# A message-passing layer on one core: one wait a step, transposes two groups ahead, destinations' rows from resident columns

## The chip, the cores and the metric

The kernel runs on 1 core of a Trainium2 chip, in float32 throughout. Five engines run their own instruction streams and meet at semaphores: TensorE (matmuls and transposes, "PE" in the profile, with its weight loads as "PEld"), VectorE ("DVE"), ScalarE ("ACT"), GpSimd ("POOL") and SyncE ("SP"). In this kernel GpSimd issues the indirect loads, and SP and ACT issue the plain ones. The metric is the device time of one execution in microseconds, median of several runs.

## What is computed

A layer of a graph network over 12,500 nodes of 64 features and 212,500 edges of 32 features, which come sorted by destination:

```python
def _mlp(x, W1, b1, W2, b2):
    return jax.nn.relu(x @ W1 + b1) @ W2 + b2
...
msg_in = jnp.concatenate([nodes[row], nodes[col], edge_features], axis=-1)   # 64 + 64 + 32
messages = _mlp(msg_in, mW1, mb1, mW2, mb2)                                  # hidden 128, out 64
aggregated = jax.ops.segment_sum(messages, col, num_segments=nodes.shape[0])
upd_in = jnp.concatenate([nodes, aggregated], axis=-1)
return _mlp(upd_in, uW1, ub1, uW2, ub2)
...
x = _layernorm(x + _L0_gnn_ref(x, src, dst, edge_attr_32, ...), axis=-1)
```

`row` is the source of an edge (`src`), `col` its destination (`dst`).

## The kernel before

The edges are cut into 554 groups of 384 (`G`, `GE`), three tiles of 128 each (`TG`; the last group has only 148 edges, in two tiles). As the edges are sorted by destination, the destinations of a group lie in a window of 32 consecutive nodes (`W`) that begins with the group's first destination. A check on the device confirms that the window holds every edge; if it does not, a slower path (`unordered`) computes everything anew. With these inputs that path does not run.

**The order is written out by hand** (`manual_schedule`): each engine runs its instructions in the order in which the program lists them. The framework adds the waits, from which instruction writes and reads which tile.

A group goes through these functions; the group a step works on is given in brackets for step g of the main loop:

- `gather` (g+16), L93 to L101: three indirect loads on GpSimd's queue, one per tile; each fetches the 64 features of 128 source nodes from HBM into the columns behind a place for a one-hot matrix in the tile `s`. There are 18 buffers of `s` (`AHEAD + 2`), so a gather has to wait until the sums of the group 18 earlier are done. The gathers also take turns on eight semaphores.
- `tables_for` (g+8) and `table`, L180 to L194: a chunk of 512 nodes at a time, the product of the nodes' features and the destinations' part of the first weight matrix (and the bias) is computed by TensorE (L184), copied by ACT (L187) and written to HBM as the table `by_dst` (L188). There are 25 such chunks (`PLAN`).
- `window` (g+4), L269 to L280: SP loads the 32 rows of `by_dst` that belong to the group's window into the first 32 rows of one of six weight tiles `wm`; below them lie, loaded once, the weights for source features (64 rows) and edge features (32 rows). The number of the window's first node is a register's value, which SP and DVE load.
- `onehot` (g+2), L282: DVE compares each edge's destination, relative to the window, with 0 to 31. That gives the one-hot columns of `s`.
- `turn` (g+1), L290: three transposes on TensorE (L298) turn one-hot and source features into columns, in PSUM (`xt`); ACT copies them to SBUF (L299), above the edge features (`st`, loaded by SP for four groups at a time, L262), and adds up how many edges each node of the window has (`counts`).
- `hidden` (g), L302: three matmuls of these 128 rows with `wm` give the hidden layer in PSUM (`pre`, L307). One-hot times table row, source features and edge features are all in the one product. ACT applies the relu (L311).
- `sums` (g−2), L317: a transpose of the counts (L321) and three matmuls of the hidden layer with the one-hot columns (L323) sum it by destination into `sg`.
- `add` (g−2), L328: DVE adds `sg` into the resident sums `agg` (L330) and the counts into row 0 of the resident `xc` (L331), at an address from the register. `xc` holds all nodes' features as columns, with the counts as its row above them.
- `step_update` (g−2), L394: as soon as all edges of a chunk of 512 nodes are through, its update (second weight matrix, update network, layer norm) is done in four parts, one per step.

Every float32 matmul shows in the profile as two passes; a transpose shows as one. In PSUM, `xt`, `pre` and `sg` have two buffers each, one bank a buffer; one more bank is for tables and updates (`u_ps`), one for a constant.

Ahead of the loop stand the loads, the preparation of the windows' starts, the first table chunk, the check, and the clearing of `agg` (L244). The first 48 gathers are issued ahead of all this, since GpSimd's stream has nothing else.

The main loop, quoted in part:

```python
for g in range(G + 2):
    if g < G:
        ...
        gather(g + AHEAD)
        tables_for(g + SOON)
        window(g + NEXT)
        onehot(g + 2)
        turn(g + 1)
        hidden(g)
    if g > 1:
        sg = sums(g - 2)
        step_update(g - 2)
        add(g - 2, sg)
```

Of the kernel before, what the change touches and what calls it, by code (L numbers as in the profile page):

```python
# [19 lines left out]
P = 128  # L20
# [14 lines left out]
NEXT = 4  # L35
# [12 lines left out]
def plan():  # L48


    import math

    def node(g, sign):
        q = min(1.0, g * GE / E)
        return g * GE * N / E + sign * (6.0 * math.sqrt((E - N) * q * (1 - q)) * N / E + 6)

    chunks, b = [], 0
    for e in [c * CH for c in range(1, N // CH + 1)] + [N]:
        opens = next((g for g in range(G) if node(g, 1) + W >= b), G)
        closes = next((g for g in range(G) if node(g, -1) >= e), G)  # L60
        n = e - b
        chunks.append((b, *((P, n // P) if n % P == 0 else (n // 2, 2)), opens, closes))
        b = e
    return chunks
# [6 lines left out]
def ordered(ctx: ExitStack, tc: tile.TileContext, a, ok):  # L71
# [6 lines left out]
    dram = ctx.enter_context(tc.tile_pool(name="dram", bufs=1, space=DRAM))  # L78
    gp = ctx.enter_context(tc.tile_pool(name="gather", bufs=AHEAD + 2))
    stp = ctx.enter_context(tc.tile_pool(name="st", bufs=3))  # L80
    bp = ctx.enter_context(tc.tile_pool(name="bout", bufs=2))
# [9 lines left out]
    gathered = {}  # L91

    def gather(g):  # L93
        s = gp.tile([P, TG, W + D], F32, name="s")
        for j, p in enumerate(tiles_of(g)):
            t = g * TG + j
            nc.gpsimd.indirect_dma_start(  # L97
                out=s[:p, j, W:], out_offset=None, in_=x[:, :],
                in_offset=bass.IndirectOffsetOnAxis(ap=src_sb[:p, t : t + 1], axis=0),
            )  # L100
        gathered[g] = s  # L101
# [14 lines left out]
    zero = const.tile([W, H], F32, name="zero")  # L116
# [5 lines left out]
    xc = const.tile([D + 1, NP], F32, name="xc")  # L122
# [4 lines left out]
    nc.sync.dma_start(xc[0:1, :].rearrange("o (p n) -> o p n", p=P), ones[:, : NP // P])  # L127
    w1b = const.tile([D + 1, H], F32, name="w1b")
    nc.scalar.dma_start(w1b[0:1, :], a["mb1"][None, :])
    nc.scalar.dma_start(w1b[1 : D + 1, :], a["mW1"][D : 2 * D, :])  # L130
    cuts = [0, 3 * CH, 12 * CH, N]
# [3 lines left out]
    NW = 6  # L135
# [9 lines left out]

    lo, hi = np.zeros(G), np.full(G, float(N - 1))
    for base, p, n, opens, closes in PLAN:
        lo[closes:] = base + p * n
        hi[:opens] = np.minimum(hi[:opens], base - W)

    def steps(v):

        at = [0, *(np.flatnonzero(np.diff(v)) + 1).tolist(), len(v)]
        return [(i, j, float(v[i])) for i, j in zip(at, at[1:])]

    bound = temp.tile([1, G], F32, name="bound")

    def set_bound(v):
        for i, j, value in steps(v):
            nc.vector.memset(bound[:, i:j], value)  # L160

    set_bound(hi)
    start_f = temp.tile([1, G], F32, name="start_f")
    nc.vector.tensor_scalar(start_f, first_f[0:1, :], 0.0, None, ALU.max)
    nc.vector.tensor_tensor(start_f, start_f, bound, ALU.min)
# [8 lines left out]


    by_dst = dram.tile([N + W, H], F32, name="by_dst")
    nc.sync.dma_start(by_dst[N:, :], zero)
    tables = list(PLAN)

    def table():  # L180
        base, p, n, _, _ = tables.pop(0)
        ps = ups.tile([H, CH], F32, name="u_ps").rearrange("p (n h) -> p n h", n=4)
        for k in range(n):
            nc.tensor.matmul(ps[:p, k], xc[:, base + k : base + p * n : n], w1b,  # L184
                             start=True, stop=True)
        t = bp.tile([P, 4, H], F32, name="t")
        nc.scalar.activation(t[:p, :n], ps[:p, :n], AF.Copy)  # L187
        nc.scalar.dma_start(  # L188
            by_dst[base : base + p * n, :].rearrange("(p n) h -> p n h", p=p), t[:p, :n])

    def tables_for(g):

        while tables and tables[0][3] <= g:
            table()  # L194

    SOON = NEXT + 4
    tables_for(SOON)

# [18 lines left out]
    nc.tensor.matmul(wps[:, 2, 0:1], u1s, b2, start=True, stop=True)  # L217
# [3 lines left out]

    nc.vector.tensor_tensor(ub1, ub1, wps[:, 2, 0:1], ALU.subtract)
# [8 lines left out]
    wrong = temp.tile([1, 2, G], F32, name="wrong")  # L231
    nc.vector.tensor_tensor(wrong[:, 0], first_f[0:1, :], bound, ALU.is_gt)
    set_bound(lo)
    nc.vector.tensor_tensor(wrong[:, 1], first_f[0:1, :], bound, ALU.is_lt)
    nwrong = temp.tile([1, 1], F32, name="nwrong")
    nc.vector.tensor_reduce(nwrong, wrong, mybir.AxisListType.XY, ALU.add)
# [13 lines left out]
    xtp = ctx.enter_context(tc.tile_pool(name="xt_ps", bufs=2, space=PSUM))  # L250
    prp = ctx.enter_context(tc.tile_pool(name="pre_ps", bufs=2, space=PSUM))
    sgp = ctx.enter_context(tc.tile_pool(name="sg_ps", bufs=2, space=PSUM))
    counts = const.tile([D + W, G], F32, name="counts")

    st, starts, hs = {}, {}, {}
# [13 lines left out]
    def window(g):  # L269
        if g >= G:  # L270
            return
        if g % SB == 0:
            n = min(SB, G - g)
            _, v = nc.values_load_multi_w_load_instructions(
                start_i[0:1, g : g + n], engines=[ET.SP, ET.DVE], min_val=0, max_val=N - 1,
                skip_runtime_bounds_check_because="they were clamped to the nodes on the chip",
            )
            for i in range(n):
                starts[g + i] = v[i]
        nc.sync.dma_start(wm[g % NW][:W, :], by_dst[bass.ds(starts[g], W), :])  # L280

# [8 lines left out]
    def turn(g):  # L290

        if g >= G:
            return
        s = gathered[g]
        t, c, n = columns(g)
        xt = xtp.tile([D + W, GE], F32, name="xt")
        for j, p in enumerate(tiles_of(g)):
            nc.tensor.transpose(xt[:, j * P : j * P + p], s[:p, j, :], ident[:p, :p])  # L298
        nc.scalar.activation(t[: D + W, c : c + n], xt[:, :n], AF.Copy,  # L299
                             accum_out=counts[:, g : g + 1])  # L300

    def hidden(g):  # L302
        t, c, n = columns(g)
        sizes = tiles_of(g)
        pre = prp.tile([P, TG, H], F32, name="pre")
        for j, p in enumerate(sizes):
            nc.tensor.matmul(pre[:p, j, :], t[:, c + j * P : c + j * P + p], wm[g % NW],  # L307
                             start=True, stop=True)
        h = ep.tile([P, TG, H], F32, name="h")
        if len(set(sizes)) == 1:  # L310
            nc.scalar.activation(h, pre, AF.Relu)  # L311
        else:
            for j, p in enumerate(sizes):
                nc.scalar.activation(h[:p, j, :], pre[:p, j, :], AF.Relu)
        hs[g] = h

    def sums(g):  # L317
        h, s = hs.pop(g), gathered.pop(g)
        sizes = tiles_of(g)
        sg = sgp.tile([P, TIMES + 1, W], F32, name="sg")  # L320
        nc.tensor.transpose(sg[0:1, TIMES, :], counts[:W, g : g + 1], ident[:W, :W])  # L321
        for j, p in enumerate(sizes):
            nc.tensor.matmul(sg[:, :TIMES, :], h[:p, j, :],  # L323
                             s[:p, j, :W].unsqueeze(1).to_broadcast([p, TIMES, W]),
                             start=j == 0, stop=j == len(sizes) - 1)
        return sg

    def add(g, sg):  # L328
        at = bass.ds(starts.pop(g), W)
        nc.vector.tensor_tensor(agg[:, at], sg[:, 0, :], agg[:, at], ALU.add)  # L330
        nc.vector.tensor_tensor(xc[0:1, at], sg[0:1, TIMES, :], xc[0:1, at], ALU.add)  # L331

    def update(base, p, n):
# [8 lines left out]
        def first(xin):  # L342
            u_ps = ups.tile([H, CH], F32, name="u_ps")
            nc.tensor.matmul(u_ps[:, :q], wc, agg[:, rows], start=True, stop=False)  # L344
            nc.tensor.matmul(u_ps[:, :q], ux, xc[:, rows], start=False, stop=True)  # L345
            u = up.tile([H, CH], F32, name="u")
            nc.scalar.activation(u[:, :q], u_ps[:, :q], AF.Relu, bias=ub1)
            nc.vector.tensor_tensor(xin[:p, :n], xin[:p, :n],
                                    u2b[:p].unsqueeze(1).to_broadcast([p, n, D]), ALU.add)
            return xin, u  # L350
# [31 lines left out]
    waiting = [(closes, update(base, p, n)) for base, p, n, _, closes in PLAN]  # L382
# [14 lines left out]
    for g in range(NEXT):  # L397
        window(g)
    onehot(0)
    onehot(1)  # L400
    turn(0)
    for g in range(G + 2):
        if g < G:
            if g % SB == 0:
                inputs(g // SB + 2)
            if g + AHEAD < G:
                gather(g + AHEAD)
            tables_for(g + SOON)
            window(g + NEXT)
            onehot(g + 2)  # L410
            turn(g + 1)
            hidden(g)
        if g > 1:
            sg = sums(g - 2)
            step_update(g - 2)
            add(g - 2, sg)
# [331 lines left out]
```

## Time and profile before

| | us |
|---|---|
| median of 3 runs (2108.9 to 2110.22) | 2109.17 |
| the profiled execution | 2528.93 |
| its span, first to last instruction | 2527.2 |
| TensorE's mean granted clock in it | 0.786 of full |
| first gather issued / last gather issued | 2.91 / 2480.53 |

The profiled execution took 420 us longer than the timed ones. The profile and its trace are of that execution.

Some further groups, in the form line, engine, operation, out<-in, shape, count | busy us, mean ns of one | idle time of the engine just before them, and what ended most of it:

```profile
L298 PE MATMUL xt<-ident,s 128*96 128x128 f32 x1661 | 355.4, 335 | 443.8 <-remote 246.7
L299 ACT ACTIVATE st<-xt 96x384 f32<-96x384 f32 x554 | 267.9, 484 | 1002.3 <-PE xt L298 469.4
L330 DVE TENSOR_TENSOR agg<-sg,agg 128x32 f32 x554 | 106.2, 192 | 1899.2 <-PE sg L323 761.2
L184 PE MATMUL u_ps<-w1b,xc 65*128 65x128 f32 (+1 forms) x196 | 54.2, 453 | 112.9 <-DVE xc L331 80.3
```

How to read them: the first says that the transposes of L298 kept TensorE busy for 355.4 us, 335 ns each, and that TensorE stood idle for 443.8 us just before such an instruction, of which 246.7 us ended with something that the trace does not name ("remote"). Idle time of an engine is no loss by itself; it is one only where the end of the kernel hangs on that engine.

### The profile page before, as it was taken

How to read it: one execution, taken by the hardware profiler on the slowest of the kernel's cores; microseconds unless marked ns; L12 is line 12 of the kernel's file. 1: busy time of each engine (PE TensorE's matmuls, PEld its weight loads, DVE VectorE, ACT ScalarE, POOL GpSimd, SP SyncE). 2: the span in 40 equal slices, each digit the busy share in tenths (PEclk: the TensorE clock that was granted, in tenths of full speed). 3: DMA queues.
4: the chain of work that ended last, by engine and by line, in shares of the span. 5: the costliest groups of instructions: out<-in, count | busy, mean ns of one | idle time of the engine just before them, and what ended most of it. 6: DMA issues, size and time to landing. Idle time of an engine off the chain costs nothing.

```text
span 2527.2 us, 31410 instructions
## 1 busy us (share of the span) xinstructions
PE 1697.3 (67%) x9359; PEld 1457.9 (58%) x9359; DVE 392.9 (16%) x2103; ACT 598.2 (24%) x1740; POOL 1570.3 (62%) x1668
## 2 busy tenths in 40 slices
PE   0566767776676776776666766666667676677667
PEld 0455656665565665665555655556566565666556
DVE  3111111111111111111111111111111111111112
ACT  0222222222222222222222222222222222222223
POOL 6666666666666666666666665666666666666661
PEclk9787777777778677777877787788787778787879
DMA  5111111111111111111111111111111111111111
GB/s 127 34 43 46 40 43 45 41 44 43 40 44 41 42 47 39 45 43 40 43 41 42 47 42 40 40 43 44 41 42 47 36 47 40 43 47 38 46 39 28
DMA packets 99895, 111.48 MB, mean 44 GB/s; under 512 B 39997, under 2 KB 65062, under 8 KB 99590
## 3 DMA queue, kind: packets, MB, share of 16 engines
q0 software_dynamic: 53152, 54.51, 9.6%
q1 hardware_dynamic: 41928, 45.07, 6.4%
q10 hardware_dynamic: 4638, 9.80, 1.3%
q8 instruction: 79, 1.29, 0.2%
q14 instruction: 98, 0.80, 0.1%
HBM read 99.55 MB, written 9.62 MB: 43 GB/s over the span
## 4 chain that ended last, share of the span: by engine, by line
PE 66%; another core or an unknown queue 16%; issue 12%; DVE 2%; ACT 1%; DVEq 0%; DMA 0%; ACTq 0%
PE sg L323 25%; PE pre L307 21%; PE xt L298 12%; PE sg L321 2%; PE u_ps L184 2%; PE u_ps L357 2%; PE u_ps L344 1%; PE u_ps L345 1%; ACT st L299 1%; DVE o L374 0%; DVE mv L364 0%; DVE stats L363 0%; DVE xc L331 0%; DVE y L359 0%
## 5 line engine op out<-in xcount | busy, mean ns | idle before, releaser
L97 POOL DMA_INDIRECT s<-in_x,src_sb x1661 | 1569.6, 945 | 910.3 <-issue 420.5
L307 PE MATMUL pre<-wm,st 128*128 128x128 f32 x3322 | 635.3, 343 | 205.1 <-issue 140.3
L307 PEld LDWEIGHTS pre<-wm,st 128*128 128x128 f32 x3322 | 572.1, 254 | 241.7 <-issue 165.3
L323 PE MATMUL sg<-s,h 128*128 128x128 f32 x3322 | 660.4, 348 | 1.8 <-issue 1.8
L298 PE MATMUL xt<-ident,s 128*96 128x128 f32 x1661 | 355.4, 335 | 443.8 <-remote 246.7
L323 PEld LDWEIGHTS sg<-s,h 128*128 128x128 f32 x3322 | 535.6, 240 | 29.2 <-issue 1.7
L298 PEld LDWEIGHTS xt<-ident,s 128*96 128x96 f32 x1661 | 234.3, 159 | 501.7 <-remote 259.2
L299 ACT ACTIVATE st<-xt 96x384 f32<-96x384 f32 x554 | 267.9, 484 | 1002.3 <-PE xt L298 469.4
L311 ACT ACTIVATE h<-pre 128x384 f32<-128x384 f32 x553 | 268.8, 486 | 668.0 <-PE pre L307 257.3
L330 DVE TENSOR_TENSOR agg<-sg,agg 128x32 f32 x554 | 106.2, 192 | 1899.2 <-PE sg L323 761.2
L285 DVE TENSOR_TENSOR s<-iota,dlc 128x96 f32<-128x96 f32 x554 | 141.9, 257 | 54.6 <-issue 53.7
L184 PE MATMUL u_ps<-w1b,xc 65*128 65x128 f32 (+1 forms) x196 | 54.2, 453 | 112.9 <-DVE xc L331 80.3
L184 PEld LDWEIGHTS u_ps<-w1b,xc 65*128 65x128 f32 (+1 forms) x196 | 47.5, 326 | 118.2 <-issue 51.9
L321 PE MATMUL sg<-ident,counts 32*1 32x32 f32 x554 | 107.2, 194 | 0.0
L299 ACT ACTIVATION_READ_ACCUMULATOR st<-xt 96x1 f32 x554 | 106.0, 191 | 0.0
L331 DVE TENSOR_TENSOR xc<-sg,xc 1x32 f32 x554 | 99.2, 179 | 13.9 <-PE u_ps L345 5.3
L321 PEld LDWEIGHTS sg<-ident,counts 32*1 32x1 f32 x554 | 41.1, 74 | 90.2 <-issue 43.9
L357 PE MATMUL u_ps<-u,u 128*128 128x64 f32 (+1 forms) x196 | 49.5, 399 | 20.5 <-issue 11.2
L357 PEld LDWEIGHTS u_ps<-u,u 128*128 128x128 f32 (+1 forms) x196 | 47.1, 324 | 23.2 <-issue 12.2
L344 PE MATMUL u_ps<-agg,wc 128*128 128x512 f32 (+1 forms) x50 | 33.3, 753 | 18.0 <-DVE agg L330 12.2
L187 ACT ACTIVATE t<-u_ps 128x512 f32<-128x512 f32 (+1 forms) x25 | 14.7, 588 | 91.3 <-issue 43.7
L366 ACT ACTIVATE rstd<-mv,eps 128x4 f32<-128x4 f32 (+1 forms) x25 | 7.4, 297 | 103.8 <-DVE mv L364 42.1
(51 smaller groups left out, 188.1 us busy)
## 6 DMA issues: line engine op xcount, KB each, us to landing
s<-in_x,src_sb POOLq DMA_INDIRECT x1661
st<-in_efT SPq DMA_DIRECT2D x138, 192.0 KB
wm<-by_dst SPq DMA_DIRECT2D x554, 16.0 KB
by_dst<-t ACTq DMA_DIRECT2D x24, 256.0 KB
xin<-in_x SPq DMA_DIRECT2D x24, 128.0 KB
out<-o SPq DMA_DIRECT2D x24, 128.0 KB
xc<-in_xT ACTq DMA_DIRECT2D x1, 1589.0 KB
xc<-in_xT ACTq DMA_DIRECT2D x1, 1152.0 KB
```

The lines of the kernel that those rows point to most:

```text
L97: nc.gpsimd.indirect_dma_start(out=s[:p, j, W:], out_offset=None, in_=x[:, :], in_offset=bass.IndirectOffsetOnAxis(ap=src_sb[:p, t : t + 1 ...
L184: nc.tensor.matmul(ps[:p, k], xc[:, base + k : base + p * n : n], w1b, start=True, stop=True)
L285: nc.vector.tensor_tensor(gathered[g][:, :, :W], iota.unsqueeze(1).to_broadcast([P, TG, W]), dlc[:, g * TG : (g + 1) * TG].unsqueeze(2).to ...
L298: nc.tensor.transpose(xt[:, j * P : j * P + p], s[:p, j, :], ident[:p, :p])
L299: nc.scalar.activation(t[: D + W, c : c + n], xt[:, :n], AF.Copy, accum_out=counts[:, g : g + 1])
L307: nc.tensor.matmul(pre[:p, j, :], t[:, c + j * P : c + j * P + p], wm[g % NW], start=True, stop=True)
L311: nc.scalar.activation(h, pre, AF.Relu)
L321: nc.tensor.transpose(sg[0:1, TIMES, :], counts[:W, g : g + 1], ident[:W, :W])
L323: nc.tensor.matmul(sg[:, :TIMES, :], h[:p, j, :], s[:p, j, :W].unsqueeze(1).to_broadcast([p, TIMES, W]), start=j == 0, stop=j == len(sizes ...
L330: nc.vector.tensor_tensor(agg[:, at], sg[:, 0, :], agg[:, at], ALU.add)
L331: nc.vector.tensor_tensor(xc[0:1, at], sg[0:1, TIMES, :], xc[0:1, at], ALU.add)
L357: nc.tensor.matmul(o_ps[:p, k], u[:, k:q:n], u2, start=True, stop=True)
```

## The change

Three things change.

- **Destinations' rows.** The table in HBM, its writing and the windows' loads go. Instead, once for every four groups, DVE copies the four windows' columns of `xc` (now with two extra rows: the counts on top, a row of ones for the bias at the bottom) side by side into a small tile `xw` (`places`), one matmul multiplies them by the weights (`windows`), and DVE copies the four blocks of 32 rows from PSUM into four of now eight weight tiles `wm`. The places are made in the steps with g mod 4 = 1, for the next four groups; the matmul and its copies follow in the steps with (g − 2) mod 4 = 0. The counts' row has weight 0 in this product.
- **One PSUM tile per step.** `xt`, `pre` and `sg` become the three banks of one tile with two buffers. Each step takes one.
- **Waits and order.** The transposes run for group g+2 instead of g+1, `onehot` for g+3. The first transpose of a group is made to depend on all of its three gathers, so that the step waits at its head; the copy of the transposes by ACT is listed behind the relu of the step.

The preparation changes with it: the bounds for the windows' starts become a clamp to the nodes, the check compares only with a lower bound, and the subtraction of a term from `ub1` goes, since the counts now start at 0 instead of 1.

```diff
-    xc = const.tile([D + 1, NP], F32, name="xc")
+    xc = const.tile([D + 2, NP], F32, name="xc")
+    nc.vector.memset(xc[:, N:], 0.0)
...
-    nc.sync.dma_start(xc[0:1, :].rearrange("o (p n) -> o p n", p=P), ones[:, : NP // P])
+    nc.sync.dma_start(xc[0:1, :].rearrange("o (p n) -> o p n", p=P), zero)
+    nc.sync.dma_start(xc[D + 1 :, :].rearrange("o (p n) -> o p n", p=P), ones[:, : NP // P])
...
-    NW = 6
+    NW = 2 * SB
...
+    def after(first, others):
+
+        for i in others:
+            tc.add_manual_dep(
+                first.ins, i.ins.name,
+                mybir.DependencyInfo(mybir.DependencyClass.Sync, mybir.DependencyReason.DATA),
+                reason="one wait for all",
+            )
...
-    xtp = ctx.enter_context(tc.tile_pool(name="xt_ps", bufs=2, space=PSUM))
-    prp = ctx.enter_context(tc.tile_pool(name="pre_ps", bufs=2, space=PSUM))
-    sgp = ctx.enter_context(tc.tile_pool(name="sg_ps", bufs=2, space=PSUM))
+
+    stepp = ctx.enter_context(tc.tile_pool(name="step_ps", bufs=2, space=PSUM))
...
-        nc.sync.dma_start(wm[g % NW][:W, :], by_dst[bass.ds(starts[g], W), :])
+        xw = xwp.tile([D + 2, SB, W], F32, name="xw")
+        for i in range(n):
+            starts[g + i] = v[i]
+            nc.vector.tensor_copy(xw[:, i, :], xc[:, bass.ds(v[i], W)])
+        xws[b] = xw, n
+
+    def windows(b, wp):
+
+
+        if b not in xws:
+            return lambda: None
+        xw, n = xws.pop(b)
+        nc.tensor.matmul(wp[: n * W, :], xw[:, :n, :], w1b, start=True, stop=True)
+
+        def copies():
+            for i in range(n):
+                nc.vector.tensor_copy(wm[(b * SB + i) % NW][:W, :], wp[i * W : (i + 1) * W, :])
+
+        return copies
...
-        xt = xtp.tile([D + W, GE], F32, name="xt")
-        for j, p in enumerate(tiles_of(g)):
+        xt = ps[: D + W, 0, :GE]
+        did = [
             nc.tensor.transpose(xt[:, j * P : j * P + p], s[:p, j, :], ident[:p, :p])
-        nc.scalar.activation(t[: D + W, c : c + n], xt[:, :n], AF.Copy,
-                             accum_out=counts[:, g : g + 1])
-
-    def hidden(g):
+            for j, p in enumerate(tiles_of(g))
+        ]
+        after(did[0], loads.pop(g)[1:])
...
     for g in range(G + 2):
+        ps = banks()
         if g < G:
             if g % SB == 0:
                 inputs(g // SB + 2)
             if g + AHEAD < G:
                 gather(g + AHEAD)
-            tables_for(g + SOON)
-            window(g + NEXT)
-            onehot(g + 2)
-            turn(g + 1)
-            hidden(g)
+            if g % SB == 1:
+                places(g // SB + 1)
+            onehot(g + 3)
+            copy = turn(g + 2, ps)
+            hidden(g, ps)
+            copy()
         if g > 1:
-            sg = sums(g - 2)
+            results = sums(g - 2, ps)
             step_update(g - 2)
-            add(g - 2, sg)
+            add(g - 2, *results)
```

## The prediction

> **What bounds the kernel now.** I read the page's busy line first, then the groups of instructions, then who waited for whom, then the timeline in four places: a pause, a steady stretch, the head and the tail.
>
> ```profile
> PE 1697.3 (67%) x9359; PEld 1457.9 (58%) x9359; DVE 392.9 (16%) x2103; ACT 598.2 (24%) x1740; POOL 1570.3 (62%) x1668
> ...
> L97 POOL DMA_INDIRECT s<-in_x,src_sb x1661 | 1569.6, 945 | 910.3 <-issue 420.5
> ```
>
> The busiest row is TensorE's, and the chain of waits gives it 66%. That would make this change, which rearranges TensorE's step, a large one. The second line says otherwise. GpSimd issues 1,661 gathers of 945 ns, and part of its idle time is called "issue", time in which it waited for nothing:
>
> ```profile
> POOL s L97 <- issue: 420.5, 1376, 0.6
> POOL s L97 <- DVE agg L330: 301.7, 152, 8.2
> ```
>
> 420.5 / 1,376 is 0.305 us behind each gather, never over 0.6. A gather therefore costs 0.945 + 0.305 = 1.250 us whatever else happens; over the gathers that did not wait, the mean distance from start to start is 1.2501 us. A group has three: **GpSimd's beat is 3.75 us a group**. The second row (waiting for a buffer that DVE's sum frees) is TensorE's lateness. Is that lateness there without the profiler? The timeline at 1,205 us:
>
> ```profile
> 1204.99 0.94 PE L323 MATMUL sg<-s,h 128*128 128x128 f32 x6
> 1206.01 0.94 POOL L97 DMA_INDIRECT s<-in_x,src_sb  x1 [0.31 <-issue]
> 1208.88 0.19 DVE L330 TENSOR_TENSOR agg<-sg,agg 128x32 f32 x1 [5.22 <-remote]
> 1209.12 0.94 POOL L97 DMA_INDIRECT s<-in_x,src_sb  x1 [2.17 <-remote]
> ```
>
> TensorE's last matmuls should end at 1205.93, but their result reaches DVE at 1208.88, with nothing in the trace to explain it ("remote"). Such pauses fill this execution: the chain gives 16% to an unknown queue. Where there is none, TensorE runs like this:
>
> ```profile
> 2486.14 0.18 PE L321 MATMUL sg<-ident,counts 32*1 32x32 f32 x1
> 2488.12 0.18 PE L321 MATMUL sg<-ident,counts 32*1 32x32 f32 x1
> ```
>
> The same instruction of two successive groups: 1.98 us, at full clock. At half the clock it is 452.20 to 455.83:
>
> ```profile
> 452.20 0.20 PE L321 MATMUL sg<-ident,counts 32*1 32x32 f32 x1
> ...
> 455.83 0.21 PE L321 MATMUL sg<-ident,counts 32*1 32x32 f32 x1
> ```
>
> 3.63 us. Both are under GpSimd's 3.75.
>
> **The sum for the kernel before.** The profiled execution took 2,528.93 us, its span 2,527.2 and 1.73 around it. GpSimd's account of the span: first gather at 2.91; 1,660 beats of 1.2501 = 2,075.2; five early waits for landings (tenth to fourteenth gather, beyond the usual 0.305) 6.8; one wait for the first free buffer 7.6 (7.87 less 0.305); 237 later waits 388.4; last gather 0.9; the rest to the end 45.8. That is 2,527.6, 0.4 over. The timed runs have a median of 2,109.17, 420 us less. Take away the 396 us of waits for buffers, and put the tail without a backlog (about 1.0 us until the last gather's packets end, then 16.2 from the last transposes at 2511.03 to the end):
>
> 2.9 + 2,075.2 + 6.8 + 0.9 + 1.0 + 16.2 + 1.7 = 2,104.7 us.
>
> The median lies 4.5 us (0.2%) above. So I read the timed runs as bound by GpSimd issuing gathers from end to end, and the profiled one as TensorE with the profiler's pauses. The 4.5 us may be a remainder of the wait for the first buffer, or a tail at half clock.
>
> **The change, part by part.** The gathers stay: same number, same shape, same buffers (18), the same two engines to wait for. So 2,075 us cannot move unless the beat does.
>
> Tables out, columns in. Away go 196 table passes on TensorE (L184: 54.2 us busy, 112.9 idle before them), 25 ACT copies (14.7 us), 25 writes to HBM, 554 reads on SP's queue. In come 139 matmuls of two passes, 278 passes at 343 ns (L307) to 453 ns (L184, the same shape): 95 to 126 us, or 0.17 to 0.23 a group. DVE gets 1,108 copies; by its nearest rows (L331 179 ns, L330 192 ns) some 205 us on 393. All of it lies beside the beat: 1.98 + 0.2 on TensorE, and DVE 598 of 2,109. I cost it at **0**; the cover is GpSimd's. If it were gone, TensorE would be at −72 us (54.2 + 112.9 − 95). SP's queue then holds only edge features, inputs and outputs; nothing waits for it more than before.
>
> One wait at the head. The first transpose of a step now waits for all three gathers of group g+2 and for the PSUM tile of two steps ago. Behind it on TensorE are hidden(g) and sums(g−2), and for these DVE's sum and GpSimd's buffer. Before, hidden(g) stood behind the transposes of g+1; so a sum now comes one beat later. gather(g+16) needs sums(g−2), which needs the landing of g+2: 14 groups, 52 us, to spare. The PSUM tile is free when DVE's sum ends, about 1.1 us after sums start (2484.16 to 2485.25), and is asked for a step later. **0** in the middle. At the end nothing hides it: after the last landing there is one more step of hidden and sums. Its price is hidden(552) to hidden(553) in the tail, 2511.40 to 2513.15 = 1.75 us; at half clock 3.63 less a group's transposes (0.65, 450.15 to 450.79) = 3.0. I take **+2.4** (1.75 to 3.0).
>
> The head. The 55th gather waits for the first DVE sum:
>
> ```profile
> 55.43 10.51 DVE L244 MEMSET agg<- 128x12544 f32 x1 [2.56 <-issue]
> ...
> 87.09 0.94 POOL L97 DMA_INDIRECT s<-in_x,src_sb  x1 [7.87 <-DVE agg L330]
> ```
>
> GpSimd would have come at 79.5; the sum ended at 87.0, of which the chain puts 7.55 and 6.48 down to pauses. Without them it is 73, in time. The change takes the first table, its round through HBM and the first four reads out of this road, and puts in eight DVE copies (1.5 us) and one matmul. Gain between 0 and the whole 4.5 us missing above. Against it, two more weight tiles and one more row are loaded in the burst in which the tenth to fourteenth gathers waited: some 0.15 MB on about 4.6, of about 24 us, +0.8. I take **−1** (−4.5 to +1.5).
>
> **A rule against the change.** The 554 new copies from `xc` to `xw` are fp32, SBUF to SBUF. The trace shows what a DVE instruction does to a gather:
>
> ```profile
> 11.18 1.89 DVE L170 TENSOR_TENSOR dlc<-dlc,first_f 128x1662 f32<-128x1662 f32 x1
> 12.26 1.63 POOL L97 DMA_INDIRECT s<-in_x,src_sb  x1 [0.30 <-issue]
> ```
>
> DVE's ends at 13.07, 0.81 into the gather, which takes 0.69 more than 0.944: the gather needs something about 0.13 us after its start, and waits if DVE holds it. The Trainium skill, "SBUF — State Buffer", section "Who interferes with whom", says that a copy in SBUF can take the port pair that DVE shares with GpSimd, and whoever comes second blocks entirely. By that rule, four copies of 0.18 us in a run that meet a gather's moment cost up to 0.18 each run: 139 runs, 25 us. By the row: L374, also fp32 SBUF to SBUF with one tensor input and in runs of four, overlapped 27 gathers after the head, and these took 0.15 us more in all (4 of them by 28 to 50 ns); over 98 instructions 1.5 ns each, 0.8 us for 554. The copies have half the elements. But runs come at a fixed phase after the gathers, since the landing starts the step, so they may meet the moment always or never. I take the row, **+1** (0 to 11, the upper end 139 hits of 0.08).
>
> Sum: +2.4 − 1 + 1 = +2.4, on 2,109.17: **2,111.5 us**. Own range, without the far end of the port: from 2,109.17 + 1.75 − 4.5 = 2,106.4, less the 1.3 over which the three runs spread, 2,105, to 2,109.17 + 3.0 + 1.5 + 2 = 2,116.
>
> **The rivals.** *The port decides, slower* (0.2): each run of copies meets the gather that is starting. Place: GpSimd, every twelfth gather; price 0.08 us on 139 runs, 11 us, so 2,121; with the rule's 25, 2,136. It decides from 20 ns a run (2.8 us): then, with the 1.4 of tail and head, the time is past the bound of 4.2. Against it: L374's row.
>
> *TensorE at half clock becomes the bound, slower* (0.04). Half-clock step 3.63, plus two passes of 0.453 in every fourth step: 3.86, over 3.75; 554 of them 2,138, and with the updates' matmuls (L344, L345, L357, 112 us) 2,250. For it: at full clock TensorE would be busy 1.98 of 3.75, and the windows of under about half busy are those after which the trace halves the clock. Against it: a wholly busy window restores it (after 452.20 the next group is at full clock), and a TensorE that is late is wholly busy. "TensorE: Matmul & The Clock Gate", Part 1, has the same: full clock after a busy window.
>
> *GpSimd is not the bound in timed runs, faster* (0.1). If the 1.250 are the profiler's as well, and TensorE's pauses are real, TensorE's 72 us count: 2,037. For it: 67% against 62%; against it: the sum that meets the median within 0.2%.
>
> **How the numbers follow.** Forecast 0.66, rivals 0.2, 0.04, 0.1. Within 0.2% (4.2 us, about what a measurement can tell from no change) is 2,105.0 to 2,113.4; of the forecast's 0.66 some 0.08 lies above. So faster 0.10, same 0.58, slower 0.32. The range reaches from a microsecond under the forecast's lower end, 2,104, to 2,109.17 + 3.0 + 1.5 + 11 = 2,125, the port's first price with tail and head at their worst; 0.1 below it and some 0.08 above are left out.
>
> **What would show it.** Gathers 1,661 times at 945 ns with 0.305 behind (over 950: the port). The 55th gather without its wait. L184 gone, 278 passes of the new matmul. One more step after the last transposes. The changed kernel's own profiled execution has pauses too and may fall by some 70 us while the timed runs stand still. I am wrong if the timed runs fall under 2,100: then the beat was not what bound them.

## The result, and the profile after

| | us |
|---|---|
| kernel before, 5 runs (2108.9 to 2110.49) | 2110.22 |
| changed kernel, 5 runs (2115.75 to 2122.68) | 2121.66 |
| ratio, 95% interval | 1.0051 [1.0036, 1.0065] |
| profiled execution of the changed kernel | 2115.75 |
| its span; mean granted clock | 2114.0; 0.936 |

The changed kernel is 0.5% slower, some 11.4 us. The forecast was 2,111.5 within 2,104 to 2,125. The range holds the time, but by luck: it reaches over 2,116 only for the port's 11 us, which did not come, and the loss came by a way that the prediction had put at 0. No change, which it held likeliest (0.58), did not come either.

From the page of the changed kernel: busy time by engine, the chain that ended last (followed back from the last instruction, at each step to what released it), and groups of instructions (busy us, mean ns of one | idle time just before them, and what ended most of it).

```profile
PE 1392.2 (66%) x9439; PEld 1197.0 (57%) x9439; DVE 620.6 (29%) x3185; ACT 552.5 (26%) x1715; POOL 1572.0 (74%) x1668
...
PE 51%; ACT 19%; DMA 12%; issue 7%; POOL 7%; DVE 3%; ACTq 0%; SPq 0%; POOLq 0%; DVEq 0%
...
L102 POOL DMA_INDIRECT s<-in_x,src_sb x1661 | 1571.2, 946 | 513.3 <-issue 370.6
...
L319 PE MATMUL ps<-ident,counts 32*1 32x32 f32 x554 | 103.5, 187 | 470.5 <-ACT st L291 469.3
...
L257 PE MATMUL ps<-w1b,xw 66*128 66x128 f32 (+1 forms) x276 | 70.7, 340 | 158.1 <-ACT st L291 158.1
```

Two things stand here. GpSimd is as forecast: 1,661 gathers of 946 ns, and its idle time has shrunk from 910.3 to 513.3 us. And there is a new wait: the counts' transpose (L319), or in every fourth step the windows' matmul (L257) ahead of it, stands for ScalarE. In the kernel before, the same transpose waited for nothing (its page, L321 there):

```profile
L321 PE MATMUL sg<-ident,counts 32*1 32x32 f32 x554 | 107.2, 194 | 0.0
```

The view of who waited for whom in the changed kernel (us in all, times, longest us) has the new wait too:

```profile
PE ps L319 <- ACT st L291: 469.3, 412, 2.1
POOL s L102 <- issue: 370.6, 1216, 0.3
PE ps L257 <- ACT st L291: 158.1, 138, 2.1
POOL s L102 <- DMA s<-in_x,src_sb: 102.0, 315, 3.4
```

412 + 138 = 550 of 554 steps wait, 627.4 us, 1.14 us each. GpSimd's row "issue" has no entry over 0.3 us, and behind the 54th gather no distance from one gather's end to the next one's start is over 0.4 us. GpSimd is therefore never held in the middle of the kernel: the new wait lies under its beat of 1.250 us a gather there. The timeline of the changed kernel (start, us, engine, line; in brackets the idle time before, and who ended it) shows what the wait is:

```profile
2078.01 0.83 PE L301 MATMUL ps<-wm,st 128*128 128x128 f32 x6
...
2078.94 0.49 ACT L305 ACTIVATE h<-ps 128x384 f32<-128x384 f32 x1 [2.60 <-PE ps L301]
2079.33 0.48 ACT L291 ACTIVATE st<-ps 96x384 f32<-96x384 f32 x1
2079.70 0.20 ACT L291 ACTIVATION_READ_ACCUMULATOR st<-ps 96x1 f32 x1
...
2079.95 0.18 PE L319 MATMUL ps<-ident,counts 32*1 32x32 f32 x1 [1.10 <-ACT st L291]
```

The hidden layer's matmuls end at 2078.84. `sums` of an older group needs nothing of this step, but writes the third bank of the tile `ps`, whose first and second bank ScalarE reads in the same step. TensorE stands 1.10 us until the relu and the copy are done. The reading on trial is that the framework orders by tile, not by bank.

Where is it paid, if GpSimd is not held? The last gather ends at 2086.07; behind it the changed kernel needs 27.95 us more. That is the place to price.

### The profile page after: what moved, and what is told of

It is laid out like the page before. It is cut to its first block, busy times and chain, and to the rows that moved or that the text cites. A ratio compares the mean times of both kernels' runs of the same rounds, so it can differ in the third digit from the quotient of the medians.

```text
span 2114.0 us, 31050 instructions
## 1 busy us (share of the span) xinstructions
PE 1392.2 (66%) x9439; PEld 1197.0 (57%) x9439; DVE 620.6 (29%) x3185; ACT 552.5 (26%) x1715; POOL 1572.0 (74%) x1668
## 4 chain that ended last, share of the span: by engine, by line
PE 51%; ACT 19%; DMA 12%; issue 7%; POOL 7%; DVE 3%; ACTq 0%; SPq 0%; POOLq 0%; DVEq 0%
PE ps L321 18%; PE ps L301 15%; DMA s<-in_x,src_sb 10%; ACT h L305 10%; ACT st L291 9%; PE ps L285 7%; POOL s L102 7%; PE ps L319 3%; PE ps L257 3%; PE u_ps L357 2%; PE u_ps L344 1%; PE u_ps L345 1%; DVE mv L364 1%; DMA ub<-in_ub 1%; DVE stats L363 1%
## 5 line engine op out<-in xcount | busy, mean ns | idle before, releaser
L102 POOL DMA_INDIRECT s<-in_x,src_sb x1661 | 1571.2, 946 | 513.3 <-issue 370.6
L305 ACT ACTIVATE h<-ps 128x384 f32<-128x384 f32 x553 | 270.5, 489 | 1303.9 <-PE ps L301 1301.6
L321 PE MATMUL ps<-s,h 128*128 128x128 f32 x3322 | 550.1, 305 | 0.0
L301 PE MATMUL ps<-wm,st 128*128 128x128 f32 x3322 | 504.9, 293 | 0.0
L301 PEld LDWEIGHTS ps<-wm,st 128*128 128x128 f32 x3322 | 457.8, 209 | 0.8
L321 PEld LDWEIGHTS ps<-s,h 128*128 128x128 f32 x3322 | 439.5, 201 | 23.7
L319 PE MATMUL ps<-ident,counts 32*1 32x32 f32 x554 | 103.5, 187 | 470.5 <-ACT st L291 469.3
L319 PEld LDWEIGHTS ps<-ident,counts 32*1 32x1 f32 x554 | 41.1, 74 | 572.2 <-ACT st L291 552.3
L285 PE MATMUL ps<-ident,s 128*96 128x128 f32 x1661 | 294.3, 289 | 35.5 <-DMA s<-in_x,src_sb 16.4
L291 ACT ACTIVATE st<-ps 96x384 f32<-96x384 f32 x554 | 264.1, 477 | 32.2 <-PE ps L285 32.1
L285 PEld LDWEIGHTS ps<-ident,s 128*96 128x96 f32 x1661 | 204.0, 137 | 63.3 <-PE ps L321 35.1
L257 PE MATMUL ps<-w1b,xw 66*128 66x128 f32 (+1 forms) x276 | 70.7, 340 | 158.1 <-ACT st L291 158.1
L261 DVE COPY wm<-ps 32x128 f32<-32x128 f32 x550 | 155.0, 282 | 5.7
L257 PEld LDWEIGHTS ps<-w1b,xw 66*128 66x128 f32 (+1 forms) x276 | 43.2, 197 | 185.7 <-ACT st L291 185.7
L291 ACT ACTIVATION_READ_ACCUMULATOR st<-ps 96x1 f32 x554 | 109.1, 197 | 0.0
```

Source lines behind the costliest of these rows:

```text
L102: nc.gpsimd.indirect_dma_start(out=s[:p, j, W:], out_offset=None, in_=x[:, :], in_offset=bass.IndirectOffsetOnAxis(ap=src_sb[:p, g * TG + ...
L257: nc.tensor.matmul(wp[: n * W, :], xw[:, :n, :], w1b, start=True, stop=True)
L261: nc.vector.tensor_copy(wm[(b * SB + i) % NW][:W, :], wp[i * W : (i + 1) * W, :])
L321: nc.tensor.matmul(sg[:, :TIMES, :], h[:p, j, :], s[:p, j, :W].unsqueeze(1).to_broadcast([p, TIMES, W]), start=j == 0, stop=j == len(sizes ...
```

## The experiments

The theory on trial, S: sharing the tile makes the first write of `sums` wait for ScalarE, about 1.17 us a step, hidden under the gathers' beat and paid behind the last gather. The rivals: X, the extra step that transposes two groups ahead leave at the end; H, the wait at the step's head; C, the destinations' rows from columns.

The twelve runs fell on three chips, four on each, and on two of these the kernel before itself takes 2,520 us. Each is compared with the kernel before on its own chip. The chip of the first comparison is not on record; its kernel before took 2,110.22, as on the first chip.

| kernel | chip | us, median (range) | kernel before | ratio, 95% interval |
|---|---|---|---|---|
| sg_own | first | 2111.94 (2109.78 to 2115.64) | 2110.84 | 1.0005 [0.9997, 1.0013] |
| act_behind | first | 2112.76 (2109.35 to 2115.7) | 2110.84 | 1.0009 [1.0001, 1.0017] |
| before_shared | first | 2124.56 (2119.95 to 2134.3) | 2110.84 | 1.0069 [1.0051, 1.0087] |
| one_ahead | first | 2119.72 (2117.14 to 2120.61) | 2110.84 | 1.0037 [1.0024, 1.005] |
| no_head_wait | second | 2851.34 (2822.39 to 2866.68) | 2521.12 | 1.125 [1.12, 1.13] |
| plain_before | second | 1389.95 (1386.59 to 1393.32) | 2521.12 | – |
| plain_after | second | 2048.61 (2045.28 to 2051.95) | 2521.12 | – |
| plain_act_behind | second | 1571.42 (1570.62 to 1572.21) | 2521.12 | – |
| after_again | third | 2851.57 (2821.28 to 2867.69) | 2517.93 | 1.1336 [1.1298, 1.1373] |
| no_head_wait_2 | third | 2853.03 (2835.2 to 2856.72) | 2517.93 | 1.1335 [1.1311, 1.1358] |
| sg_own_2 | third | 2486.52 (2485.14 to 2488.99) | 2517.93 | 0.9878 [0.9858, 0.9899] |
| columns_only | third | 2484.4 (2483.96 to 2486.69) | 2517.93 | 0.9868 [0.9845, 0.9891] |

### The sums in a tile of their own

```diff
+    sgp = ctx.enter_context(tc.tile_pool(name="sg_ps", bufs=2, space=PSUM))
...
-        return stepp.tile([P, 3, 512], F32, name="ps")
+        return stepp.tile([P, 2, 512], F32, name="ps")
...
-        sgw = ps[:, 2, : (TIMES + 1) * W + H]
+        sgw = sgp.tile([P, 512], F32, name="sg")[:, : (TIMES + 1) * W + H]
```

> The changed kernel, but the sums get a PSUM tile of their own again (two buffers, one bank each); transposes and hidden layer still share one. Theory S (the first write of the sums into the shared tile waits until ScalarE has read the step's other banks, about 1.17 us a step, hidden under GpSimd's beat of 3.75 us and visible behind the last gather): that wait goes, TensorE's step at full clock falls from 3.31 to about 2.15 us, and the time to 2,110 to 2,115 us. Rival X (the extra step at the end, from transposes two groups ahead): no change, 2,119 to 2,123. Rival C (the rows made from resident columns: DVE's copies and the extra matmul): no change, 2,119 to 2,123. Rival H (the wait at the step's head): no change.

Measured: 2,111.94 beside 2,110.84. Three lines undo the loss, while columns, two groups ahead and the wait at the head all stay. Lines of its page, the chain and two groups:

```profile
DMA 37%; PE 22%; POOL 22%; issue 15%; DVE 3%; POOLq 0%; SPq 0%; ACT 0%; DVEq 0%; ACTq 0%
...
L286 PE MATMUL ps<-ident,s 128*96 128x128 f32 x1661 | 309.3, 300 | 611.1 <-DMA s<-in_x,src_sb 513.4
...
L320 PE MATMUL sg<-ident,counts 32*1 32x32 f32 x554 | 104.2, 188 | 0.0
```

The counts' transpose no longer waits at all (0.0 against 470.5 us), so the wait was the tile's; and TensorE's idle time is now in front of the transposes, for landings: it is ready before the gathers are. ScalarE's share of the chain goes from 19% to 0%.

The loss itself is seen in the tails. The changed kernel first, its TensorE alone; the first line is the last group's transposes:

```profile
2091.62 0.61 PE L285 MATMUL ps<-ident,s 128*96 128x128 f32 x2
2092.16 1.65 PE L301 MATMUL ps<-wm,st 128*128 128x128 f32 x6
2094.77 0.21 PE L319 MATMUL ps<-ident,counts 32*1 32x32 f32 x1 [0.96 <-ACT st L291]
2094.91 1.65 PE L321 MATMUL ps<-s,h 128*128 128x128 f32 x6
2096.35 1.49 PE L301 MATMUL ps<-wm,st 128*128 128x128 f32 x6
2098.48 0.18 PE L319 MATMUL ps<-ident,counts 32*1 32x32 f32 x1 [0.64 <-ACT h L305]
...
2100.65 0.18 PE L319 MATMUL ps<-ident,counts 32*1 32x32 f32 x1 [0.57 <-ACT h L308]
...
2102.72 0.90 PE L321 MATMUL ps<-s,h 128*128 128x128 f32 x4
```

The same stretch of the version with the sums' own tile:

```profile
2089.30 0.42 PE L286 MATMUL ps<-ident,s 128*96 128x128 f32 x2
2089.65 0.94 PE L302 MATMUL ps<-wm,st 128*128 128x128 f32 x6
2090.52 0.18 PE L320 MATMUL sg<-ident,counts 32*1 32x32 f32 x1
...
2092.95 0.18 PE L320 MATMUL sg<-ident,counts 32*1 32x32 f32 x1
...
2096.56 0.90 PE L322 MATMUL sg<-s,h 128*128 128x128 f32 x4
```

Their last gathers end at 2086.07 and 2085.90. From there to the last transposes it is 5.55 against 3.40 us: in both kernels the update of the last full chunk lies there, in the changed one a wait of 1.10 us too. From those to the end of the last sums it is 12.00 against 8.16. Three waits make 2.2 us of this, and three blocks of six passes at or near half clock another 2.0 (1.65, 1.65 and 1.49 us instead of 0.94, 0.94 and 0.91). The last update then takes 10.4 against 10.6. Together 27.95 against 22.16: **5.8 us** between these two executions, waits and slower clock together.

### ScalarE's reads listed behind the sums

```diff
-            nc.scalar.activation(h, pre, AF.Relu)
+        def relu():
+            nc.scalar.activation(h, pre, AF.Relu)
...
-            hidden(g, ps)
-            copy()
+            relu = hidden(g, ps)
         if g > 1:
             results = sums(g - 2, ps)
+        if g < G:
+            relu()
+            copy()
```

> The changed kernel with its shared PSUM tile kept, but ScalarE's relu and copy are listed behind the matmuls of the sums, so that the sums have no reader of the tile ahead of them. Theory S: the wait for ScalarE ahead of the sums goes as with PSUM tiles apart, 2,110 to 2,115 us; the copy comes later, but is needed only a step later. If sharing costs something by itself (two buffers of three banks, freed together), this stays at 2,119 to 2,123 while tiles apart gain. Rivals X, C and H: no change.

Measured: 2,112.76, ratio 1.0009. The shared tile stays and nearly all of the loss goes, so it hung on the order of reader and writer in a step.

### The kernel before with a shared tile

```diff
-        xt = xtp.tile([D + W, GE], F32, name="xt")
+        xt = ps[: D + W, 0, :GE]
...
-        pre = prp.tile([P, TG, H], F32, name="pre")
+        pre = ps[:, 1, : TG * H].rearrange("p (j h) -> p j h", h=H)
...
-        sg = sgp.tile([P, TIMES + 1, W], F32, name="sg")
+        sg = ps[:, 2, : (TIMES + 1) * W].rearrange("p (t w) -> p t w", w=W)
...
-            turn(g + 1)
-            hidden(g)
+            copy = turn(g + 1, ps)
+            hidden(g, ps)
+            copy()
```

> The kernel before, with table in HBM, transposes one group ahead and no wait at the head, but with its three PSUM tiles made the three banks of one tile per step and ScalarE's copy listed behind the relu. Theory S: the same wait appears ahead of the sums, about 1.2 us a step, and the time rises by 5 to 10 us, to 2,115 to 2,121. Rivals X, C and H: as before, 2,108 to 2,112.

Measured: 2,124.56, +13.7 us, more than expected. The tile and the copy behind the relu alone, put into the kernel before, bring the loss; C, X and H are not in this kernel. Its counts' transpose now waits as in the changed kernel:

```profile
L326 PE MATMUL ps<-ident,counts 32*1 32x32 f32 x554 | 104.0, 188 | 614.5 <-ACT st L302 614.0
```

### Transposes one group ahead

```diff
-    for g in range(2):
+    for g in range(1):
         turn(g, banks())()
...
-            copy = turn(g + 2, ps)
+            copy = turn(g + 1, ps)
```

> The changed kernel with the transposes one group ahead instead of two; all else stays. Theory S: one step less behind the last landing, but with the wait for ScalarE still in it, so 2 to 4 us less than the changed kernel: 2,117 to 2,120. Rival X (all of the loss is the extra step): back to 2,109 to 2,112. Rivals C and H: no change, 2,119 to 2,123.

Measured: 2,119.72, ratio 1.0037 beside the changed kernel's 1.0051: 2 to 3 us less, with intervals that overlap. X is at most a small part. Its tail, TensorE alone, shows something else:

```profile
2097.81 0.21 PE L319 MATMUL ps<-ident,counts 32*1 32x32 f32 x1 [0.91 <-ACT st L291]
2097.95 1.65 PE L321 MATMUL ps<-s,h 128*128 128x128 f32 x6
...
2101.28 1.65 PE L321 MATMUL ps<-s,h 128*128 128x128 f32 x6
```

Here TensorE runs at half clock from 2097.81 to the end. The five traces of these kernels fall into two kinds:

| kernel | behind the last gather, us | granted clock from there to the end of the last sums |
|---|---|---|
| changed kernel | 27.95 | 0.81 |
| before_shared | 32.56 | 0.77 |
| one_ahead | 29.31 | 0.71 |
| sg_own | 22.16 | 1.00 |
| act_behind | 22.58 | 1.00 |

The three with the wait end at a lower clock, the two without it at full clock. That goes together; that the waits bring the clock down is not shown. A longer stretch at half clock is a possible reason why the changed kernel's other runs lie 4 to 7 us above the profiled one, which was the fastest of five; they have no trace here, so this is not shown either.

### Without the wait at the head

```diff
-        after(did[0], loads.pop(g)[1:])
+        loads.pop(g)
```

> The changed kernel without the dependency that makes a step's first transpose wait for all three gathers; the shared PSUM tile and two groups ahead stay. Theory S: no change against the changed kernel, 2,118 to 2,123, for the wait ahead of the sums stays. Rival H (the loss is the step held at its head until the last of three gathers has landed): back to 2,109 to 2,113.

It fell on the second chip: 2,851.34 where the kernel before takes 2,521.12. Alone that says nothing of H, so it was run again beside the changed kernel:

> The changed kernel without the dependency that holds a step's first transpose until all three gathers have landed. Theory S: within 2 us of the changed kernel beside it where the kernel before takes 2,110, and within 3% of it where that takes 2,520. Rival H: 8 us below it, back at the kernel before.

> The changed kernel once more, beside the next three. On a chip where the kernel before takes about 2,110 us: 2,116 to 2,123 again, for the wait for ScalarE ahead of the sums shows behind the last gather alone. On a chip where the kernel before takes about 2,520 us, TensorE pauses there and falls behind GpSimd's beat, so the 1.17 us a step count in full steps: 2,700 to 2,900.

Measured on the third chip: 2,853.03 without the wait, 2,851.57 with it. The wait does not explain the loss there, but the runs of one kernel spread by 20 to 46 us, so the 8 us of rival H could not be seen. On the first chip it was not tried by itself; there sg_own and act_behind keep the wait and have next to no loss, and before_shared has the loss without it. That is what rules H out.

On these chips the loss is 13% (on the second, measured without the wait at the head alone). Waits of the changed kernel on the third:

```profile
POOL s L102 <- PE ps L321: 687.6, 291, 10.1
ACT h L305 <- remote: 671.9, 105, 14.8
...
PE ps L319 <- ACT st L291: 658.2, 304, 7.8
```

The second row is made of pauses that the trace does not name, the same as in the profiled execution of the kernel before. They leave TensorE behind the gathers, GpSimd waits for it (first row), and then the 1.1 us at the head of `sums` are no longer covered. At half clock the step with the wait is over GpSimd's 3.75 us; two successive groups of no_head_wait on the second chip, 4.82 us apart:

```profile
1203.13 0.21 PE L319 MATMUL ps<-ident,counts 32*1 32x32 f32 x1 [4.02 <-ACT h L305]
...
1207.95 0.20 PE L319 MATMUL ps<-ident,counts 32*1 32x32 f32 x1 [1.10 <-ACT st L291]
```

### The parts of the change where TensorE is the bound

sg_own again, and the first part of the change alone:

> The sums in a PSUM tile of their own, once more. Theory S: where the kernel before takes 2,110, again 1 to 3 us above it; where that takes 2,520 and TensorE is behind, the lost time comes back in full: between 2,400 and 2,550, some 300 us below the changed kernel.

```diff
-        xt = ps[: D + W, 0, :GE]
+        xt = xtp.tile([D + W, GE], F32, name="xt")
...
-        pre = ps[:, 1, : TG * H].rearrange("p (j h) -> p j h", h=H)
+        pre = prp.tile([P, TG, H], F32, name="pre")
...
-            copy = turn(g + 2, ps)
-            hidden(g, ps)
-            copy()
+            turn(g + 1, ps)()
+            hidden(g, ps)
```

> Only the first part of the change: destinations' rows from resident columns; three PSUM tiles, transposes one group ahead with ScalarE's copy right behind them, no wait at the head. Theory S: no loss is left, 0 to 2 us below sg_own by the step that is not behind the last landing, so 2,108 to 2,111 where the kernel before takes 2,110; where that takes 2,520, some 2 to 4% less than it by the table's passes that are gone. Rival C (DVE's copies and the extra matmul are what costs): 5 to 10 us above the kernel before.

Measured on the third chip, beside 2,517.93: the columns alone 2,484.4 (−33.5 us, 1.3%, less than the 2 to 4% expected); with the shared tile for transposes and hidden layer, two groups ahead and the wait at the head 2,486.5 (+2.1); with the sums' bank in the shared tile 2,851.6 (**+365**, 0.66 us a step of the 1.17). The columns are a small gain where TensorE is late, and one bank of PSUM outweighs it ten times.

### With most of GpSimd's beat taken away

In three kernels only the first tile of a group is gathered; the other two are plain loads of consecutive rows, issued by SP, so that two thirds of the gather by source are left out:

```diff
+            if j:
+                nc.sync.dma_start(s[:p, j, W:], x[(g * GE + j * P) % (96 * P) :, :][:p])
+                continue
```

> The kernel before, but only the first of a group's three tiles is gathered by source; the other two come by plain loads of consecutive rows of the nodes (left out: two thirds of the gather by source). GpSimd's beat falls from 3.75 to 1.25 us a group, so TensorE's step is no longer covered. Both theories: 554 steps of 1.98 us, 112 us of updates, 167 of tables, some 95 for head and tail, 1,350 to 1,500 us. If the time stays near 2,110, GpSimd was not what set it.

> The changed kernel with the same two plain loads a group (left out: two thirds of the gather by source). Theory S: each step carries the wait for ScalarE, 554 x 1.17 = 648 us, against some 72 us that the tables' way out gives back: 500 to 650 us longer than the kernel before with the same loads. Rivals X and H: an extra step or a wait at the head costs once, or nothing, so within 100 us of the kernel before with the same loads.

> The version with ScalarE's relu and copy behind the sums, with the same two plain loads a group (left out: two thirds of the gather by source). Theory S: the wait is gone and the tables' way out counts, so 0 to 150 us below the kernel before with the same loads. Rivals: like the changed kernel with these loads.

Measured, with two runs of each: 1,389.95, 2,048.61 and 1,571.42. The changed kernel is 658.7 us longer than the kernel before with the same loads, 1.19 a step and a little over the 500 to 650 expected. The counts' transposes of successive groups, first in plain_before:

```profile
801.66 0.18 PE L324 MATMUL sg<-ident,counts 32*1 32x32 f32 x1
803.64 0.18 PE L324 MATMUL sg<-ident,counts 32*1 32x32 f32 x1
```

and in plain_after:

```profile
800.07 0.18 PE L320 MATMUL ps<-ident,counts 32*1 32x32 f32 x1 [1.10 <-ACT st L292]
803.22 0.18 PE L320 MATMUL ps<-ident,counts 32*1 32x32 f32 x1 [1.10 <-ACT st L292]
```

1.98 us a group at full clock before, 3.15 after: +1.17, as in S. X, which costs once, cannot make that; nor can H, since the transposes at the step's head (L286) waited 1.6 us in all in plain_after.

The third kernel was expected at or below plain_before and is 181 us above it. Its steps alternate between 1.98 and about 3.1 us; at the head of one of the long ones:

```profile
800.44 0.20 ACT L292 ACTIVATION_READ_ACCUMULATOR st<-ps 96x1 f32 x1
...
800.70 0.50 PE L286 MATMUL ps<-ident,s 128*96 128x128 f32 x3 [1.11 <-ACT st L292]
```

With ScalarE's reads behind the sums, the tile comes free only when they end, and the transposes at the head of a step wait for that: part of the wait has moved rather than gone. Of the edits tried, only a tile of their own for the sums left none. No version tried is faster than the kernel before on the first chip; on the third, columns_only and sg_own lie 2.1 us apart, less than the runs of either spread.

## Why the prediction was right or wrong

**The bound: right for the timed runs, wrong about the profiled one.** The changed kernel's gathers run at 946 ns with 0.305 behind, unheld after the head, as forecast. But the prediction called the pauses in the profiled execution "the profiler's". They go with the chip: on the second and third the kernel before took 2,510 to 2,531 us in all 22 runs, and its profiled execution of 2,528.93 is like these; on the first chip profiled executions have no such rows. So the rival in which "TensorE's 72 us count" has its place there: on the third chip the columns gave 33.5 of them.

**Tables out, columns in, 0: right.** sg_own carries this part and stands at 1.0005.

**One wait at the head: the failed step.** The prediction gave the shared tile one sentence: it "is free when DVE's sum ends, about 1.1 us after sums start, ... and is asked for a step later". That follows the tile from one use of a buffer to the next, and not within the step: transposes and hidden layer write two banks, ScalarE reads them, and only then comes the write of the sums to the third. The diff shows both halves, the one tile and the order relu, copy, sums. "0 in the middle" held on the first chip, for the reason given, GpSimd's cover. The end, "+2.4 (1.75 to 3.0)", counted one more step but no longer steps; the tail was 5.8 us longer than with tiles apart, and the median 11.4. For the extra step itself, one_ahead gives back 2 to 3 us of median, which fits but is not clear of noise.

**The head, −1: nothing that can be told.** The 55th gather's wait of 7.87 us is gone, but the change did not take it: before_shared on the first chip has the tables and no such wait either, and on the third chip the changed kernel's 55th gather stands 10.08 us. The early landing waits sum to 6.0 us against 6.8, and to 8.5 in before_shared: single executions.

**The port, +1: about right.** After the head a gather takes 943.97 ns on average, before 943.52: 0.7 us in all. The 554 new copies lengthened no gather beyond 955 ns. They did not simply miss its moment: 57 were running from 0.12 to 0.15 us after a gather's start, and these gathers took 944.1 ns on average. What lengthens a gather shows again in sg_own's timeline, with an addition that was there before the change:

```profile
2080.97 0.42 DVE L349 TENSOR_TENSOR xin<-xin,u2b 128x256 f32<-128x256 f32 x1
2081.11 1.09 POOL L102 DMA_INDIRECT s<-in_x,src_sb  x1 [0.30 <-issue]
```

DVE ends at 2081.39, 0.28 into the gather, which takes 0.15 longer: 0.28 less the 0.13 of the prediction. But holding that moment is not enough. In the kernel before, four of these additions began 0.02 to 0.06 us after a gather's start and ran 0.4 us on, and the gathers took 944 to 945 ns; those that an addition lengthened found it at least 0.06 us old. None of the 57 copies was 0.05 us old when its gather began, so how an older one would act stays open. The Trainium skill, "SBUF — State Buffer", section "Who interferes with whom", says that a DVE instruction with two inputs in SBUF contends with a GpSimd instruction that reads SBUF, and that the order of issue decides who blocks. The additions agree with it, save that the gather loses only DVE's stretch behind that moment.

**TensorE at half clock as the bound: priced too low.** The estimate of the half-clock step was 3.86 us; with the wait it is 4.8. On the first chip no gather was held by it; on the other two GpSimd waited for TensorE. Its rule of the clock holds in one direction only. In the trace of the kernel before, cut into the 3.41 us in which the granted clock changes, behind the first 100 us, 140 of the 141 stretches at full clock that were under 0.47 busy were followed by half clock, but so were 30 of the 256 busier ones.

## What to carry to other kernels

In this framework a tile shared by several stages makes a write wait for the earlier readers of its other parts: walk through one step in program order and name, for each write to the tile, who has read it just before. A wait hidden under another engine's beat is not free; it comes out behind the last work of that engine (5.8 us here between two executions), and step by step wherever the waiting engine is the bound (365 us on the third chip, 659 with plain loads). Keep PSUM banks that different engines read in tiles of their own, unless the order puts the readers off the next writer's path.

## What was not expected of the hardware

The chips differ by far more than the change. The kernel before takes 2,110.84 us on the first, 2,521.12 and 2,517.93 on the second and third, with granted clocks of 0.90 to 0.91 against 0.77 to 0.79. Each chip was measured at one time only, so chip and time cannot be told apart. On the latter two, results of TensorE reach DVE and ScalarE microseconds late without a cause in the trace. In sg_own on the third chip, from the view of waits:

```profile
ACT h L306 <- remote: 1114.7, 160, 12.4
DVE agg L329 <- remote: 874.5, 152, 31.4
```

The same kernel has no such row on the first chip; nor have the three kernels with plain loads on the second, where the clock was 0.962 to 0.997 in the profiled executions. What causes the pauses, and why the kernels with plain loads have none, stays open.
